# Two graph layers on one core: POOL's large operations in pieces, a played order, and the loads' place in their queue

## The chip, the cores and the metric

The kernel runs on one core of a Trainium2 chip. The metric is the device time of one execution in microseconds (us), as the median of several runs. The core has five engines that work side by side, each through its own instructions in order: PE (matrix multiplications), DVE (vector operations), ACT (activations and copies), POOL (a second, slower vector engine) and SP, which here issues transfers. Engines wait for each other through semaphores.

## The reference

A batch of 128 graphs with 128 nodes each has node features x (64 numbers) and an adjacency matrix adj. Two layers follow each other, each with a residual and a normalization:

```python
# layer 0
mask = (adj > 0.0)
xj_proj = x @ W1[:F]
diff = x[:, :, None, :] - x[:, None, :, :]
h = relu(xj_proj[:, :, None, :] + diff @ W1[F:] + b1)     # F = 64, H = 192
hm = einsum('bjkh,bjk->bjh', h, mask)
deg = sum(mask, axis=-1)
x = layernorm(x + hm @ W2 + deg[..., None] * b2)
# layer 1
agg = einsum('bmn,bnd->bmd', adj, x)
h = elu(agg @ V1 + c1)
h = elu(h @ V2 + c2)
x = layernorm(x + h @ V3 + c3)
```

About 6% of adj is positive, so a node has few neighbours, and h is needed for those alone.

## The kernel before, in words

Graphs are worked on in 64 pairs. For a pair the kernel sorts the nodes by degree and gives each block of nodes (BLOCKS) as many neighbour slots as its largest node should need. The slots of a pair make nine units of 66 to 170 columns. A dense path at the end (`dense`) takes pairs with larger degrees than the slots allow; on these inputs it only looks whether there are any.

For each pair p these steps are generators, run as threads:

- `load` issues two transfers on SP's queue (adj and xx, L498 and L500), three pairs ahead (AHEAD).
- `prepare` makes the mask mk and the degrees on DVE (L511), degb and keyc on POOL (L518, L519), spreads them on PE (L524, L526), ranks them (cmp, L533) and makes the permutation permb (L541) on DVE.
- `sort_x` makes permf on ACT (L552), sorts x on PE (L556), copies it to xsT (L560), projects it (L570) and adds the bias to make aj (L577, ACT). POOL then makes sa (L584) and corr (L603); between them stand a product on PE (L589, L591) and ea on DVE (L596).
- `sort_mask` sorts the mask on PE (L612, L615), copies it on ACT (mtp L620, permT L622), takes prefix sums (L626), copies them to vp (L629) and makes the one-hot matrices oh on DVE (L636), one for each unit.
- `turn` transposes adj and x on PE (L651, L652) and copies them (turned, L656). `project_c` projects (L669, L672) and splits the result cp into three bf16 parts: ACT makes the first (L679), DVE the rest r (L683), ACT the second (L686), POOL the third (L688).
- `unit`, nine times, copies aj into one of four PSUM banks e (L811, ACT), gathers onto it on PE with 18 matmuls (L823) and reduces it to sums on DVE (L832). It is the bulk of the work.
- `finish` makes hm on POOL (L741), projects it (L746 to L753), brings it back to the order of the nodes (ys L757, L763), normalizes it to x (y L696, st L701 on DVE; ve L708, rs L709, nb L712 on POOL; apply L719 on ACT), aggregates (L770, agg L774) and runs layer 1 (L778 and L780, L786 and L787, L792 and L794, with exponentials e L729 on ACT and h L732 on DVE) up to the last normalization and the transfer of o (L798).

Sorting, gathering and aggregating are matmuls of 64 columns, marked "PE:t"; the others use all 128.

The order of all instructions is made when the program is built, by `Flow`. It keeps a clock for each engine, and for a resource called PORT that POOL's operations and oh on DVE both take. A thread offers its next step with a planned cost and the events that it needs; a step can be issued from the time when all of them are there. Among the steps for the engine of the earliest one that could start within NEAR (NEAR_PE on PE) of it, `Flow` takes the one with the smallest due time. A change of mode on PE adds SWITCH to the planned time and HOLD to the due time. The due time of a thread starts at `due(p, step)` = ROUND (p - AHEAD) + STEP step and grows by STEP with each step; units use PACE = ROUND / 9, and are also held to it by the time at which the first one ran (T0). Due times only choose among steps: on the chip there are no clocks, only the order and the semaphores.

Four further PSUM banks m are handed out by `Flow` for everything else. The constants have threads of their own: `arrive` (weights on ACT's queue), `arrive_next` (b1, b2 on SP), `arrive_late` (seven transfers of v2, v3, v1 and the biases on SP, L236), `consts_pool` (slotc L351, srow L357, v1p L360), `consts_dve`, `consts_w` (wc L398, L403, the sums copy L405, the product L411, L414), `consts_b2` (POOL, L328 to L332) and `consts_late` (w2d L452, v1p L457, slots L463, L471, rows L474 and on). Before the threads run, the loads of pairs 0 to 2 are issued, then `arrive_late`, and only then do the first lanes start, which issue the load of pair 3.

Of the kernel before, what the change touches and what calls it, by code (L numbers as in the profile page):

```python
# [87 lines left out]
class Flow:  # L88
# [11 lines left out]
    NEAR_PE = 0.05  # L100
    SWITCH = 0.1
    HOLD = 5
# [8 lines left out]
    def start(self, due, pace, gen):  # L111

        self.serial += 1
        th = [due, self.serial, pace, gen, None]
        self._next(th, None)

    def _next(self, th, got):
        try:
            th[4] = th[3].send(got)
        except StopIteration:  # L120
            if th in self.threads:
                self.threads.remove(th)
            return
        if th not in self.threads:
            self.threads.append(th)
        elif got is not None:
            th[0] += th[2]
# [50 lines left out]
def sparse(tc, env):  # L178
# [6 lines left out]
    NE = 4  # L185
# [7 lines left out]
    ROUND = 11.39  # L193
    AHEAD = 3
    PACE = ROUND / NB
    STEP = 1.94
    TURN = 4
    CS = 3
    SORT = 5
    FIN = 0.5  # L200

    def due(p, step):
        return ROUND * (p - AHEAD) + STEP * step

    def pace(u):
        return PACE * u

# [25 lines left out]
    const, temp = g.const, g.const  # L233

# [72 lines left out]
    def arrive_next():  # L307
        halves(nc.sync, b1c, g.b1, [[1, HB], [HB, 3]])
        fetch(b2r, bass.AP(tensor=g.b2.tensor, offset=g.b2.offset, ap=[[0, P], [1, O]]))
        happened([6.0], "const", "b1")  # L310
        happened([6.0], "const", "b2")

    def arrive_late():
        fetch(v2s, g.v2)
        fetch(v3s, g.v3)
        for s in range(2):
            fetch(v1d[s * F:(s + 1) * F], g.v1)
        for c, lo, times in ((g.c1, 0, 1), (g.c2, H1, 1), (g.c3, 2 * H1, 2)):
            n = c.shape[0]
            fetch(rows[:, lo:lo + times * n].rearrange("p (t n) -> p t n", t=times),  # L320
                  bass.AP(tensor=c.tensor, offset=c.offset, ap=[[0, P], [0, times], [1, n]]))
        happened([14.0], "const", "v")
        happened([14.0], "const", "c")
# [12 lines left out]
    def consts_pool():  # L336
# [11 lines left out]
        flow.start(0.1, 0.1, consts_prefix(below))  # L348
        yield from op("POOL", 0.2, lambda: v.memset(b2p, 0.0), "b2p0")
# [8 lines left out]
        yield from op("POOL", 1.0, scale, "srow")  # L358
        for s in range(2):
            yield from op("POOL", 0.3, lambda: v.memset(v1p[:, s], 0.0), f"v1p0{s}")  # L360
# [9 lines left out]
    def consts_dve():  # L370
# [8 lines left out]
        yield from op("DVE", 0.4, lambda: v.memset(wad, 0.0), "wad0")  # L379

# [121 lines left out]
    def prepare(p):  # L502
# [42 lines left out]
        flow.start(due(p, SORT), STEP, sort_x(p, ev))  # L545
        flow.start(due(p, SORT), STEP, sort_mask(p, ev))

# [16 lines left out]
    def project_a(p, xsT, ev):  # L564
# [19 lines left out]
        evs, = yield ("POOL PORT", 0.95, [have] + made("srow"), 0, lambda: nc.gpsimd.tensor_mul(sa, aj, srow))  # L584
# [18 lines left out]
        ev, = yield ("POOL PORT", 1.05, [ev, evs], 0, lambda: nc.gpsimd.tensor_sub(corr, ea, sa))  # L603
# [41 lines left out]
    def turn(p):  # L645

        d, a, xx = S[p], ADJ[p], XX[p]

        def transpose(t):
            for s in range(2):  # L650
                nc.tensor.transpose(t[:, s * N:(s + 1) * N], a[:, s, :], ident)  # L651
            nc.tensor.transpose(t[:, 2 * N:3 * N], flat(xx), ident)  # L652
        ev, t = yield ("PE", 0.4, [event("load", p)] + made("ident"), 1, transpose)
        turned = d["turned"] = prep.tile([P, 3, N], F32, name="turned", bufs=9)
        ev, = yield ("ACT", act(3 * N), [ev], 0,
                     lambda: nc.scalar.copy(flat(turned), t[:, :3 * N]))  # L656
        flow.give(t, ev)
        happened(ev, "turned", p)
        flow.start(due(p, CS), STEP, project_c(p, ev))

    def project_c(p, ev):
# [19 lines left out]
        for s in range(2):  # L681
# [5 lines left out]
        ev, = yield ("POOL PORT", 1.12, [ev], 0,  # L687
                     lambda: nc.gpsimd.tensor_sub(cp[:, 2], r1, cp[:, 1]))  # L688
# [47 lines left out]
    def finish(p):  # L736
# [3 lines left out]
        ev, = yield ("POOL PORT", 1.05, [event("corr", p)] + [event("sums", p, i) for i in range(NB)], 0,  # L740
                     lambda: nc.gpsimd.tensor_sub(hm, d["sums"], d["corr"]))  # L741
# [97 lines left out]
    def begin(p):  # L839
        if p < NP:  # L840
            load(p)
            happened([max(flow.clock.values(), default=1.0 + p) + 2.5], "load", p)
            flow.start(due(p, 0), STEP, prepare(p))
            flow.start(due(p, TURN), STEP, turn(p))
# [3 lines left out]
    def lane(u, ev):  # L848
        p = units[u][0]
        if p not in begun:  # L850
            begun.add(p)
            begin(p + AHEAD)
            flow.start(ROUND * (p + FIN), STEP, finish(p))
        ev = yield from unit(u, ev)
        if u + NE < len(units):
            flow.start(pace(u + NE), PACE, lane(u + NE, ev))

    nc.vector.memset(mone, -1.0)
    for p in range(min(AHEAD, NP)):
        begin(p)  # L860
        if p == 0:
            arrive_next()
    arrive_late()
    flow.start(-101.0, 0.1, arrive())
    flow.start(-100.0, 0.1, consts_pool())
    flow.start(-99.0, 0.1, consts_dve())
    flow.start(-98.0, 0.1, consts_w())
    flow.start(-97.0, 0.1, consts_wad())
    flow.start(-96.0, 0.1, consts_b2())
    flow.start(-95.0, 0.1, consts_banks())  # L870
    flow.start(ROUND * -0.5, 1.0, consts_late())
    for k in range(NE):
        flow.start(pace(k), PACE, lane(k, [0.0]))
# [217 lines left out]
```

## Time and profile before

| | us |
|---|---|
| median of 3 runs | 790.31 (789.89 to 790.33) |
| the profiled execution | 789.11 |
| its span in the trace | 787.3 |
| PE busy | 756.4 (96%) |
| DVE busy | 736.8 (94%) |
| ACT busy | 661.6 (84%) |
| POOL busy | 441.7 (56%) |
| gathers, L823 on PE | 376.4, 10368 matmuls |
| reductions, L832 on DVE | 345.6, 576 operations |
| oh, L636 on DVE | 168.3, 576 operations |
| cp, L688 on POOL | 74.8, 64 operations of 128x512 |
| hm, sa, corr (L741, L584, L603) on POOL | 64.3, 64.1, 64.0, 64 operations of 128x384 each |

A busy time is the time in which an engine works on something; what lies between the span and it is idle time, for which the trace names the event that ended it. PE's ends are modelled, so distances between starts say more about PE than durations do. Tables by stretches give, for each engine, the busy time within a stretch of the span. The chain of work that ended last is 91% PE.

### The profile page before, as it was taken

The page shows a single profiled execution, that of the slowest core. Times are in us where ns is not written, and L with a number is a line of the kernel's source. Part 1 is how long each engine was busy: PE and PEld are TensorE (multiplying, and loading weights), DVE is VectorE, ACT ScalarE, POOL GpSimd, SP SyncE. Part 2 cuts the span into 40 slices and gives each one's busy share as a digit, 9 for nine tenths or more (in the row PEclk, how much of TensorE's full clock was granted, in tenths as well). Part 3 has the DMA queues.
Part 4 walks back from the last instruction along what each step waited for, and adds up shares of the span by engine and source line. Part 5 has one row for each costly group of instructions (what it writes and reads, how often), then busy time and mean ns, then how long its engine had stood idle before and what let it go on. Part 6 is the DMA issues. An engine that isn't in the chain of part 4 may idle for free.

```text
span 787.3 us, 35836 instructions
## 1 busy us (share of the span) xinstructions
PE 756.4 (96%) x14551; PEld 684.9 (87%) x14552; DVE 736.8 (94%) x2421; ACT 661.6 (84%) x1862; POOL 441.7 (56%) x806
## 2 busy tenths in 40 slices
PE   4889999999999999999999999999999999999994
PEld 2578999999999999999999999999999999999983
DVE  3899999999999999999999999999999999999982
ACT  1868889898989989898998989889898988989862
POOL 4445556555655655565565556556556655655542
PEclk9999999999999999999999999999999999999996
DMA  3000101101101110110111011011101101110000
GB/s 95 2 2 23 27 22 27 30 20 30 26 20 30 27 29 20 30 27 20 30 27 29 21 30 26 20 30 26 30 20 31 26 20 30 27 28 21 9 9 14
DMA packets 63884, 19.91 MB, mean 25 GB/s; under 512 B 46560, under 2 KB 63712, under 8 KB 63712
## 3 DMA queue, kind: packets, MB, share of 16 engines
q1 hardware_dynamic: 63008, 17.25, 9.4%
q8 instruction: 116, 1.90, 1.0%
q14 instruction: 56, 0.46, 0.2%
q10 hardware_dynamic: 704, 0.30, 0.1%
HBM read 13.27 MB, written 4.19 MB: 22 GB/s over the span
## 4 chain that ended last, share of the span: by engine, by line
PE 91%; DVE 4%; ACT 1%; DMA 1%; issue 1%; SPq 1%; POOL 1%; ACTq 0%; POOLq 0%; DVEq 0%
PE e L823 43%; PE m L570 6%; PE m L746 6%; PE m L669 5%; PE m L780 4%; PE m L794 4%; PE m L787 4%; PE m L763 4%; PE m L770 2%; PE m L556 2%; PE m L651 2%; PE m L750 1%; PE m L672 1%; PE m L589 1%; DVE sums L832 1%; DVE oh L636 1%
## 5 line engine op out<-in xcount | busy, mean ns | idle before, releaser
L823 PE MATMUL e<-oh,cp 128*64 128x162 bf16 (+3 forms) x10368 | 376.4, 228 | 5.4 <-ACT e L811 3.8
L823 PEld LDWEIGHTS <-cp 128*64 128x64 bf16 x10368 | 349.1, 110 | 24.4 <-issue 16.9
L832 DVE TENSOR_REDUCE sums<-e 128x54 f32<-128x486 f32 (+8 forms) x576 | 345.6, 610 | 4.2 <-PE e L823 1.9
L811 ACT COPY e<-aj 128x504 f32<-128x504 f32 (+6 forms) x576 | 300.2, 549 | 17.0 <-DVE sums L832 11.6
L636 DVE TENSOR_TENSOR oh<-vp,slotc 128x336 bf16<-128x336 bf16 (+6 forms) x576 | 168.3, 321 | 0.7 <-PE e L823 0.5
L688 POOL TENSOR_TENSOR cp<-r,cp 128x512 bf16<-128x512 f32 x64 | 74.8, 1170 | 73.8 <-ACT cp L686 73.7
L709 POOL TENSOR_TENSOR rs<-ve,mhalf 128x2 f32<-128x2 f32 x128 | 89.2, 697 | 10.6
L577 ACT ACTIVATE aj<-m,b1c 128x128 f32<-128x128 f32 x192 | 56.5, 365 | 34.7 <-PE m L570 34.6
L741 POOL TENSOR_TENSOR hm<-sums,corr 128x384 f32<-128x384 f32 x64 | 64.3, 1004 | 31.1 <-DVE sums L832 31.1
L518 POOL CAST degb<-deg 128x2 bf16<-128x2 f32 x64 | 12.4, 193 | 122.5 <-DVE mk L511 122.5
L584 POOL TENSOR_TENSOR sa<-aj,srow 128x384 f32<-128x384 f32 x64 | 64.1, 1001 | 15.6 <-ACT xsT L560 8.3
L603 POOL TENSOR_TENSOR corr<-ea,sa 128x384 f32<-128x384 f32 x64 | 64.0, 1001 | 11.2 <-DVE ea L596 11.2
L679 ACT CAST cp<-m 128x256 bf16<-128x256 f32 x128 | 41.6, 376 | 33.3 <-PE m L672 33.2
L729 ACT ACTIVATE e<-m,mone 128x256 f32<-128x256 f32 x128 | 60.7, 474 | 6.7 <-PE m L787 3.7
L708 POOL TENSOR_SCALAR ve<-st 128x2 f32<-128x2 f32 x128 | 24.5, 191 | 67.1 <-DVE st L701 61.6
L732 DVE SCALAR_TENSOR_TENSOR h<-e,m 128x256 f32<-128x256 f32 x128 | 53.0, 414 | 5.5 <-ACT e L729 5.5
L570 PE MATMUL m<-xsT,wad 128*128 128x128 f32 x384 | 57.6, 287 | 0.5 <-DVE h L732 0.5
L746 PE MATMUL m<-w2d,hm 128*128 128x128 f32 x384 | 54.3, 278 | 0.0
L683 DVE TENSOR_TENSOR r<-m,cp 128x256 f32<-128x256 f32 x128 | 48.5, 419 | 5.8
L719 ACT ACTIVATE x<-y,nb,rs 128x64 f32<-128x64 f32 x128 | 51.1, 464 | 0.9 <-POOL nb L712 0.8
L570 PEld LDWEIGHTS m<-xsT,wad 128*128 128x128 f32 x384 | 48.7, 194 | 0.9 <-DVE h L732 0.7
L746 PEld LDWEIGHTS m<-w2d,hm 128*128 128x128 f32 x384 | 48.0, 192 | 1.1 <-POOL hm L741 0.2
(147 smaller groups left out, 1416.6 us busy)
## 6 DMA issues: line engine op xcount, KB each, us to landing
adj<-in_adj_dram SPq DMA_DIRECT2D x64, 128.0 KB, 2.4
xx<-in_x_dram SPq DMA_DIRECT2D x64, 64.0 KB, 2.1
out_dram<-o SPq DMA_DIRECT2D x64, 64.0 KB, 1.6
degs<-ys SPq DMA_DIRECT2D x64, 1.0 KB, 1.6
w1s<-in_L_gnn_W_dram ACTq DMA_DIRECT2D x2, 96.0 KB, 3.1
rows<-in_L_gnn_b_dram SPq DMA_DIRECT2D x3, 64.0 KB, 3.4
w2s<-in_L_gnn_W_dram ACTq DMA_DIRECT2D x2, 48.0 KB, 2.7
v2s<-in_L_gnn_W_dram SPq DMA_DIRECT2D x1, 64.0 KB, 2.3
```

The lines of the kernel that those rows point to most:

```text
L570: nc.tensor.matmul(aps[:, c * N:(c + 1) * N], wad[:, c, :], xsT, start=True, stop=True)
L584: evs, = yield ("POOL PORT", 0.95, [have] + made("srow"), 0, lambda: nc.gpsimd.tensor_mul(sa, aj, srow))
L603: ev, = yield ("POOL PORT", 1.05, [ev, evs], 0, lambda: nc.gpsimd.tensor_sub(corr, ea, sa))
L636: lambda: nc.vector.tensor_tensor(oh[:, :, c].rearrange("p b (s w) -> p b s w", w=w), vp[:, :, p0:p1].rearrange("p b (o w) -> p b o w", o= ...
L688: lambda: nc.gpsimd.tensor_sub(cp[:, 2], r1, cp[:, 1]))
L709: nc.gpsimd.tensor_tensor(rs, ve, mhalf, op=OP.pow)
L729: lambda: nc.scalar.activation(e, z, AF.Exp, bias=mone))
L741: lambda: nc.gpsimd.tensor_sub(hm, d["sums"], d["corr"]))
L746: nc.tensor.matmul(yb[:, :2 * O], hm[:, c, :], flat(w2d[:, c]), start=(c == 0), stop=False)
L811: lambda: nc.scalar.copy(e.rearrange("p (c s w) -> p c s w", c=3, w=w), d["aj"][:, :, p0:p1].rearrange("p c (o w) -> p c o w", o=1) .to_br ...
L823: nc.tensor.matmul(e[s * HB:(s + 1) * HB, c * n:(c + 1) * n], cp[:, k, s, c * HB:(c + 1) * HB], oh[:, s, base:base + n], start=False, stop ...
L832: nc.vector.tensor_reduce(d["sums"][:, :, p0:p1], e.rearrange("p (c s w) -> p c w s", c=3, w=w), AX.X, OP.add, apply_absolute_value=True)
```

## The change

It has five parts.

1. POOL's four large operations of a pair are issued in pieces: sa, corr and hm (384 columns) in three of 128, the third part of cp (2 x 256 columns) in four of 128. Each piece is a step of its own, with a planned cost of 0.42 in place of 0.95 to 1.12.
2. The due times come from a table DUE, one number for each step of each kind of thread, counted from ROUND p; ROUND goes from 11.39 to 11.21. A thread no longer has a due time that grows evenly. NEAR_PE goes from 0.05 to 0.03 and HOLD from 5 to 4.9.
3. The planned arrival of a load comes from a running clock of SP's queue (`queued`) instead of a fixed distance from the engines' clocks.
4. `arrive_late`, the seven transfers of late constants, is issued after the first lanes have started, so behind the load of pair 3.
5. Of the constants' threads, those for slotc, srow, b2p and v1p on POOL, and those from mtwoh on on DVE, become threads of their own with later due times; the memset of b2p comes after srow.

What is computed stays as it is. The diff, cut to its core:

```diff
-    NEAR_PE = 0.05
+    NEAR_PE = 0.03
     SWITCH = 0.1
-    HOLD = 5
+    HOLD = 4.9
...
-    def start(self, due, pace, gen):
+    def start(self, base, due, gen):
 
         self.serial += 1
-        th = [due, self.serial, pace, gen, None]
+        th = [0.0, self.serial, gen, iter(due), None, base]
         self._next(th, None)
...
+        th[0] = th[5] + next(th[3], th[0] - th[5])
         if th not in self.threads:
             self.threads.append(th)
-        elif got is not None:
-            th[0] += th[2]
...
-    ROUND = 11.39
+    ROUND = 11.21
...
+    DUE = {
+        "prepare": (-34.01, -32.27, -30.23, -29.85, -25.33),
+        "sort_x": (-13.14, -15.45, -7.19, -8.98, -19.88, -5.52, -3.51, -2.52, 0.83, 1.06, 7.6,
+                   4.57, 6.95),
...
+        "finish": (15.58, 20.81, 18.39, 20.56, 21.58, 23.28, 25.11, 26.72, 28.25, 29.18, 28.09,
+                   29.43, 35.25, 38.97, 38.77, 39.45, 41.87, 43.65, 44.61, 47.29, 53.63, 49.35,
+                   55.17),
+        "unit": (0, -6.28, 2.48),
+    }
...
+    def begin_thread(name, p, gen):
+        flow.start(ROUND * p, DUE[name], gen)
...
+    SP = [0.7]
+
+    def queued(cost):
+
+        SP[0] = max(SP[0], max(flow.clock.values(), default=0.0)) + cost
+        return [SP[0] + 2.6]
...
-        evs, = yield ("POOL PORT", 0.95, [have] + made("srow"), 0, lambda: nc.gpsimd.tensor_mul(sa, aj, srow))
+
+        for c in range(3):
+            evs, = yield ("POOL PORT", 0.42, [have] + made("srow"), 0,
+                          lambda: nc.gpsimd.tensor_mul(sa[:, c], aj[:, c], srow[:, c]))
...
-        ev, = yield ("POOL PORT", 1.05, [ev, evs], 0, lambda: nc.gpsimd.tensor_sub(corr, ea, sa))
+        for c in range(3):
+            evs, = yield ("POOL PORT", 0.42, [ev, evs], 0,
+                          lambda: nc.gpsimd.tensor_sub(corr[:, c], ea[:, c], sa[:, c]))
...
-        ev, = yield ("POOL PORT", 1.12, [ev], 0,
-                     lambda: nc.gpsimd.tensor_sub(cp[:, 2], r1, cp[:, 1]))
+        for s in range(2):
+            for h in range(2):
+                part = slice(h * cols // 2, (h + 1) * cols // 2)
+                evl, = yield ("POOL PORT", 0.42, [ev], 0,
+                              lambda: nc.gpsimd.tensor_sub(cp[:, 2, s, part], r1[:, s, part],
+                                                           cp[:, 1, s, part]))
...
-        ev, = yield ("POOL PORT", 1.05, [event("corr", p)] + [event("sums", p, i) for i in range(NB)], 0,
-                     lambda: nc.gpsimd.tensor_sub(hm, d["sums"], d["corr"]))
+        have = [event("corr", p)] + [event("sums", p, i) for i in range(NB)]
+        for c in range(3):
+            ev, = yield ("POOL PORT", 0.42, have, 0,
+                         lambda: nc.gpsimd.tensor_sub(hm[:, c], d["sums"][:, c], d["corr"][:, c]))
...
             load(p)
-            happened([max(flow.clock.values(), default=1.0 + p) + 2.5], "load", p)
-            flow.start(due(p, 0), STEP, prepare(p))
-            flow.start(due(p, TURN), STEP, turn(p))
+            happened(queued(1.0), "load", p)
+            begin_thread("prepare", p, prepare(p))
+            begin_thread("turn", p, turn(p))
...
-    arrive_late()
-    flow.start(-101.0, 0.1, arrive())
...
-    for k in range(NE):
-        flow.start(pace(k), PACE, lane(k, [0.0]))
+    flow.start(-101.0, [0.0], arrive())
...
+    for k in range(NE):
+        flow.start(pace(k), DUE["unit"], lane(k, [0.0]))
+    arrive_late()
     flow.run()
```

## The prediction

> **What bounds the kernel now.** I read the page's busy shares first (PE 96%, DVE 94% of 787.3 us), then the busy time of the engines by stretches, cut where PE's idle time changes. After the two times of a stretch come the busy times of PE, weight loads, DVE, ACT and POOL.
>
> ```profile
> 0.00:9.10 9.10, 5.50 (x20) 2.89 (x21) 5.51 (x41) 2.35 (x5) 7.69 (x41) 1.00 0.48 115
> 9.10:16.20 7.10, 0.03 (x1) 0.00 (x0) 0.75 (x4) 0.48 (x1) 0.27 (x2) 1.00 0.42 109
> 16.20:33.50 17.30, 15.00 (x107) 10.47 (x107) 11.71 (x51) 11.92 (x39) 5.22 (x10) 1.00 0.02 4
> 33.50:60.00 26.50, 21.69 (x472) 18.74 (x474) 26.00 (x78) 18.00 (x46) 12.99 (x15) 1.00 0.01 3
> 60.00:100.00 40.00, 39.36 (x743) 35.55 (x739) 38.22 (x126) 34.48 (x97) 23.16 (x43) 1.00 0.11 26
> 100.00:745.00 645.00, 644.91 (x12742) 592.08 (x12739) 631.11 (x2067) 574.53 (x1627) 379.36 (x673) 1.00 0.11 25
> 745.00:764.70 19.70, 19.20 (x426) 17.88 (x421) 17.62 (x44) 13.65 (x34) 6.59 (x12) 1.00 0.07 13
> 764.70:787.30 22.60, 10.70 (x63) 7.26 (x61) 5.87 (x19) 6.24 (x18) 6.38 (x15) 0.67 0.06 13
> ```
>
> From 100 to 745 us PE is idle for 0.09 us: a round of one pair takes 11.49 us (the same row of the timeline returns at that distance) and PE is its only bound, DVE being at 631.11/645 = 97.8%. The change leaves PE's matmuls as they are. So it can win only what PE loses at the ends: 3.6 + 7.1 + 2.3 + 4.8 + 0.6 us up to 100 us, and 12.4 us after 745. The largest piece, 9.1 to 16.2 us, has a name in the list of waits:
>
> ```profile
> PE m L651 <- DMA adj<-in_adj_dram: 8.5, 2, 7.1
> DVE mk L511 <- DMA adj<-in_adj_dram: 8.7, 4, 6.3
> ```
>
> Third column: the longest wait, 7.1 us, for the adj of pair 3. The timeline of SP's queue says why it is late:
>
> ```profile
> 5.85 0.47 SPq L500 DMA_DIRECT2D xx<-in_x_dram  x1
> 6.37 0.47 SPq L236 DMA_DIRECT2D v2s<-in_L_gnn_W_dram  x1
> 6.88 0.43 SPq L236 DMA_DIRECT2D v3s<-in_L_gnn_W_dram  x1
> 7.35 1.14 SPq L236 DMA_DIRECT2D v1d<-in_L_gnn_W_dram  x2
> 8.53 1.53 SPq L236 DMA_DIRECT2D rows<-in_L_gnn_b_dram  x3
> 10.11 0.47 SPq L498 DMA_DIRECT2D adj<-in_adj_dram  x1
> ```
>
> Seven constants are issued ahead of pair 3. Its transposes stand early in PE's in-order queue, with L411 and the keys of pair 0 (L524) behind them, so pair 0 itself waits for pair 3. In the stretch 33.5 to 60 the bound is another: DVE is busy 26.0 of 26.5 us and PE loses 4.8.
>
> The rows for POOL and its port:
>
> ```profile
> L688 POOL TENSOR_TENSOR cp<-r,cp 128x512 bf16<-128x512 f32 x64 | 74.8, 1170 | 73.8 <-ACT cp L686 73.7
> L329 POOL TENSOR_TENSOR hm<-b2r,hi 128x64 f32<-128x64 f32 x1 | 0.3, 307 | 0.0
> ```
>
> ```profile
> 32.20 2.50 POOL L688 TENSOR_TENSOR cp<-r,cp 128x512 bf16<-128x512 f32 x2 [2.75 <-ACT cp L686]
> 32.52 1.17 DVE L636 TENSOR_TENSOR oh<-vp,slotc 128x336 bf16<-128x336 bf16 x1
> ```
>
> The second pair is the lock: an oh takes a median of 0.32 us, but 1.17 when it starts inside POOL's cp.
>
> **What the skill says.** "SBUF — State Buffer", section "SBUF: two separate sides": DVE operations with two SBUF inputs and POOL operations share a port pair, as an exclusive lock held for the whole instruction. The trace agrees (the 1.17 us above). "GPSIMD Engine Reference", section 3.1: a two-input operation on POOL costs about 2.6 cycles an element; at the 1.2 GHz that the section reckons with, an estimate of 0.83 us for 384 columns. The trace has 1.001, so some 0.17 is fixed, and shorter pieces pay it more often. "TensorE: Matmul & The Clock Gate", Part 1: PE starts at half its clock and warms after about 3.4 us of sustained work. The trace agrees in kind: six matmuls of L570 take 1.59 us at 23.4 and 0.89 at 26.5.
>
> **The change, part by part.** Sums are made against the profiled execution: span 787.3, own time 789.1, which is 1.2 below the median of 790.3; I subtract the same difference from the median.
>
> *Loads' order and the start.* The order of instructions of the new kernel has load 3 right behind load 2, so its adj is issued at 6.37 in place of 10.11. Adj of pairs 1 and 2 landed 3.0 and 2.9 us after issue (4.35 to 7.33, 5.34 to 8.2), so I expect it at 9.3. The seven constants move back by two issues (1.0 us). Who waits for them: v1p on ACT, which now stands between xsT and vp of pair 0, near 13.5 us, while v1d should be in by 9.5 + 3.0 = 12.5; L471 on PE and L474 on DVE come later. I take 0, at most 1.0 if v1d is late, since vp is behind it. PE's queue now has L411 and the keys of pair 0 ahead of the transposes of pairs 1 to 3. The chain by old durations: sums copy ends about 7.45 (DVE has prefix, wc 0.40, wad 0.70, mk 0.4, w2d 0.69, copy 0.54 from 4.7 on), L411 1.54, wc 0.22, keys and their latency 0.5, cmp 0.54, permb 0.5: permb of pair 0 near 11.2 against 20.2. POOL's degb of pair 0 moves ahead of the v1p and b2p constants (7.07 to about 6.3), and mk moving behind wc and wad is hidden, as POOL's slotc runs until 5.8. From permb to the first complete gather was 20.2 to 33.5, 13.3 us. It then falls near 23 to 25. But PE reaches it with one L669 and one L570 fewer done (0.70 + 0.67), so not all of 9 is gained. As DVE bounds the ramp, I check with its account: DVE idle before 60 us was 3.6 + 6.3 + 5.6 + 0.5 = 16.0. In the new chain I count 4.1 of waits up to 14.5 us (0.8 before its first operation, 0.7 for w1s, 1.5 for L411, 1.1 for the keys of pairs 0 to 2 and vp of pair 0) and allow 3.4 for later ones (vp of pair 1, cp of pair 0): 7.5. Gain 8.5, from 6 to 11.
>
> *Pieces.* Thirteen POOL operations replace four. Each: between 1.001/3 = 0.33 (no fixed part) and, from the rows of 64 and 384 columns, 0.307 + 64 x 2.17 ns = 0.45. I take 0.45. Per pair 13 x 0.45 = 5.8 against 1.17 + 3 x 1.00 = 4.2, so POOL goes from 441.7/64 = 6.9 to 8.5 of 11.4 us: 74%, hidden beside PE. A blocked oh loses at most 0.45 instead of 0.85. In the ramp three were blocked (32.5, 36.8, 70.8), for 2.5 us of a bound DVE: gain 1.0, from 0 to 1.5. Between 100 and 745 no oh was blocked, so there is nothing to gain there.
>
> *Order in the round.* Counting changes between 64-column and full matmuls in the new order, there are four in a round as before, about 0.1 us each by start distances. The gathers go 5 and 4 together in place of 8 and 1, which leaves more time to refill the four e banks. One wait of 0.054 us after L570 in each old round (start to start 0.723 for 0.670) may go: -3.1 over 57 rounds. New waits are possible. The tightest that I find by laying the old durations along the new order: x of layer 0 is ready at about 8.35 us of the round and PE wants it at 8.55 (L770); the bank for L570 is free 0.4 ahead. What is queued behind L770 is the whole of PE. I take -0.5; from -3 to +12, the last being 0.2 a round.
>
> *Tail.* The last pair's chain after its last gather was 22.6 us. In the new order PE's work behind the last gather, by steady start distances, is 2 x 0.90 (L746 to L753) + 2 x 0.45 + 2 x 0.22 + 3 x 0.55 + 4 x 0.54 + 4 x 0.50 = 8.95, against 6.0 before. 2.9 us of other pairs' work moves under a chain that leaves PE idle for half its time, so the last gather comes that much sooner; the two last pairs now interleave, which I price at 0.9. Gain 2.0, from 0 to 2.9. NEAR_PE and HOLD act on the order alone and are contained in it.
>
> Sum: -8.5 - 1.0 - 0.5 - 2.0 = -12.0: 777.1 for the profiled execution, 778.3 for the median.
>
> **Rivals.** *The round grows* (slower): more POOL instructions, each with its own wait, make x's factors or an oh late in every round, and PE stands at L770. For it: x's 0.2 us of slack, POOL at 74%, factors of 1.64 us in the trace (ve, rs, nb) where the kernel plans 1.24. Against it: hm and cp have over 1 us, and DVE has 2% spare. The other 12 us are eaten from 12/57 = 0.21 us a round; at 0.4 it is 778.3 + 23 = 801. *The start is given back*: DVE, busy 26.0 of 26.5 in the ramp, keeps PE waiting whatever came earlier; start and pieces give 3, tail 2: 785.3. *It does nothing*: the wait for adj is only the first of several and L411, b2p or vp end at the old time; 790.
>
> **How the numbers follow.** Forecast 0.66, round grows 0.14, start given back 0.14, nothing 0.06. A measurement of this kernel can tell about 0.2% (1.6 us) from no change. Faster 0.66 + 0.14 = 0.80, same 0.06, slower 0.14. The range: low from the gains at their ends (11 + 1.5 + 3 + 2.9 = 18.4 gives 771.9, cut to 773), high to 788.5, past the rival at 785 and short of the other two.
>
> **What would show it.** Right: adj of pair 3 issued near 6.4, no PE wait over 2 us after 8 us, first gather complete by 25, PE idle for under 0.2 us between 100 and 745, last gather to end 22 to 24 us. Wrong: rounds over 11.6 us with PE waiting at L770 for ACT or at L746 for POOL; or DVE full and PE losing over 8 us between 25 and 60.

## The result, and the profile after

| us | before | after |
|---|---|---|
| median | 790.21 (789.89 to 790.33, 4 runs) | 785.09 (784.65 to 787.08, 4 runs) |
| ratio, 95% interval | | 0.9941, 0.9923 to 0.9959 |
| the profiled execution | 789.11 | 785.48 |
| its span | 787.3 | 783.6 |
| PE busy | 756.4 (96%) | 764.4 (98%) |
| PE idle (span less busy) | 30.9 | 19.3 |
| POOL busy | 441.7 (56%) | 527.6 (67%) |
| one round (median distance of the same row) | 11.494 | 11.663 |

The kernel became 5.1 us faster by the medians (3.6 between the two profiled executions, of which the one before lies 1.1 below its median); 12.0 were forecast. The table says where the rest is. PE's idle time fell by 11.6 us, nearly what the forecast had in sum. But PE's busy time rose by 8.0 us, though it does the same 14551 matmuls. The difference of the two is that of the spans, 3.7 us (the last digit is rounded).

These are the stretches of the kernel after, cut as before (the last stretch ends 0.36 us behind the span); after the two times come PE, weight loads, DVE, ACT and POOL.

```profile
0.00:9.10 9.10, 5.41 (x23) 3.43 (x25) 5.98 (x38) 1.87 (x4) 6.61 (x34) 1.00 0.47 116
9.10:16.20 7.10, 6.33 (x48) 5.13 (x47) 5.71 (x37) 5.48 (x18) 3.64 (x15) 1.00 0.29 75
16.20:33.50 17.30, 15.88 (x226) 12.16 (x224) 14.48 (x49) 13.43 (x38) 8.04 (x18) 0.80 0.03 9
33.50:60.00 26.50, 25.22 (x500) 21.44 (x500) 25.95 (x82) 19.80 (x51) 16.18 (x43) 1.00 0.10 25
60.00:100.00 40.00, 40.00 (x771) 36.00 (x772) 39.11 (x130) 35.69 (x102) 27.39 (x71) 1.00 0.09 21
100.00:745.00 645.00, 644.99 (x12555) 581.30 (x12550) 629.43 (x2039) 566.24 (x1602) 448.75 (x1161) 1.00 0.11 25
745.00:764.70 19.70, 19.66 (x409) 18.14 (x405) 15.83 (x38) 13.38 (x34) 11.55 (x30) 1.00 0.05 9
764.70:784.00 19.30, 6.87 (x42) 4.52 (x41) 5.16 (x17) 6.25 (x19) 5.46 (x14) 0.74 0.08 19
```

Up to 100 us PE is idle for 7.2 us (3.69 + 0.77 + 1.42 + 1.28 + 0), where it was 18.4. The hole of 7.1 us is gone. Behind 745 us it is idle for 12.1 (0.04 + 12.43, less the 0.36), nearly as before (12.4). The sixth line is the surprise: PE is full in both kernels, but in the same 645 us the kernel after gets through 12555 matmuls, the kernel before through 12742. A full engine can still be slower; the busy share doesn't show it. A matmul of L595 stands in the trace with 275 ns, while the next one starts 112 ns behind it, so a gap of 0.1 us between two starts is covered and counts as busy.

The queue of SP has the load of pair 3 where it was expected, ahead of the constants:

```profile
6.23 0.47 SPq L523 DMA_DIRECT2D adj<-in_adj_dram  x1
...
7.26 0.47 SPq L252 DMA_DIRECT2D v2s<-in_L_gnn_W_dram  x1
```

How the lead comes and goes is seen from the ends of the 576 reductions (L832 before, L870 after), after less before: the first -8.9 us, the 36th -13.6, the 54th -12.8, the 301st -10.4, the 501st -6.8, the last -4.8. So the start won 12.8 up to the 54th, the rounds gave back 8.0, and the end behind the last reduction is 1.2 longer (23.0 for 21.8).

**Where the round grew.** As ends of matmuls are modelled, I go by distances between starts, from the first matmul of a group to the first of the next. Each group has a distance that it takes when a group of its own form follows; what is more is the price of the change or a wait. The form stands in the lines: 128*128 is a full matmul, 128*64 one of 64 columns, 64*128 one of 64 rows. This is one run of full matmuls of the kernel after, on PE:

```profile
300.73 0.42 PE L581 MATMUL m<-permf,xx 128*64 128x128 f32 x4
301.08 0.23 PE L830 MATMUL m<-rowp,onesb 128*128 128x128 bf16 x1
...
301.60 0.61 PE L801 MATMUL m<-ys,permT 128*128 128x64 f32 x4
302.14 0.70 PE L700 MATMUL m<-wc,turned 64*128 64x256 f32 x4
...
303.40 0.87 PE L595 MATMUL m<-xsT,wad 128*128 128x128 f32 x6
304.20 0.90 PE L861 MATMUL e<-oh,cp 128*64 128x168 bf16 x20
```

And this is where project_c stood in the kernel before, directly behind the 64-column gathers:

```profile
401.57 0.97 PE L823 MATMUL e<-oh,cp 128*64 128x162 bf16 x32
402.46 0.70 PE L669 MATMUL m<-wc,turned 64*128 64x256 f32 x4
```

project_c's first part (L700, before L669) is neither full nor of 64 columns: it is the only step of 64 rows, which the description of the kernel doesn't name as a form of its own. Behind gathers it takes part in a change that is due anyway. Behind L801 it makes one of its own: L801 to L700 is 540 ns, and L801 takes 447 when a full matmul follows (L763 to L570 in the kernel before). The table has the medians over some 54 rounds, in ns:

| change | before | after |
|---|---|---|
| 64-column steps to the first run of full matmuls | L823 to L669: 402 - 286 = 116 | L581 to L830: 356 - 220 = 136 |
| to project_c inside a run | none | L801 to L700: 540 - 447 = 93 |
| first run to gathers | L615 to L823: 205 - 112 = 93 | last matmul of L595 to L861: 205 - 110 = 95 |
| 64-column steps to the second run | L823 to L589: 783 - 655 = 128 | L808 to L549: 356 - 220 = 136 |
| second run to gathers | L652 to L823: 202 - 109 = 93 | L646 to L861: 205 - 112 = 93 |
| sum | 430 | 553 |

(286, 655 and 220 are the distances of the same gathers and of the fp32 steps L581 and L808 when a step of 64 columns follows. The change back from 64 rows to full matmuls, L669 to L672 and L700 to L703, takes 635 ns in both kernels and is left out.) The difference is 123 of the 169 ns. Beside it, weights that are loaded late cost 39 ns at L595 and 33 at L784, each between the first matmul of the group and the second. At L595 the first weights are loaded 43 ns behind the signal of y on DVE, which gives back a bank; what L784 waits for isn't shown. In the kernel before, the step of L595 (there L570) lost 53 ns at the same place, the step of L784 (L746) nothing. That makes 19 ns more, and small differences add 27.

### The profile page after: what moved, and what is told of

The parts are those of the page before. It is cut to its first block, busy times and chain, and to the rows that moved or that the text cites. A ratio compares the mean times of both kernels' runs of the same rounds, so it can differ in the third digit from the quotient of the medians.

```text
span 783.6 us, 36480 instructions
## 1 busy us (share of the span) xinstructions
PE 764.4 (98%) x14551; PEld 682.1 (87%) x14552; DVE 741.7 (95%) x2421; ACT 662.1 (84%) x1862; POOL 527.6 (67%) x1382
## 4 chain that ended last, share of the span: by engine, by line
PE 94%; DVE 2%; DMA 1%; ACT 1%; POOL 0%; issue 0%; SPq 0%; ACTq 0%; POOLq 0%
PE e L861 44%; PE m L595 6%; PE m L784 6%; PE m L700 5%; PE m L818 4%; PE m L801 4%; PE m L832 4%; PE m L825 3%; PE m L581 2%; PE m L808 2%; PE m L682 2%; PE m L549 2%; PE m L788 1%; PE m L703 1%; PE m L830 1%; PE m L657 1%
## 5 line engine op out<-in xcount | busy, mean ns | idle before, releaser
L849 ACT COPY e<-aj 128x504 f32<-128x504 f32 (+6 forms) x576 | 315.6, 560 | 62.2 <-DVE sums L870 60.7
L861 PE MATMUL e<-oh,cp 128*64 128x162 bf16 (+3 forms) x10368 | 365.2, 228 | 0.5 <-DVE oh L667 0.3
L861 PEld LDWEIGHTS <-cp 128*64 128x64 bf16 x10368 | 344.0, 110 | 16.3 <-issue 1.4
L870 DVE TENSOR_REDUCE sums<-e 128x54 f32<-128x486 f32 (+8 forms) x576 | 345.5, 610 | 8.3 <-PE e L861 1.6
L722 POOL TENSOR_TENSOR cp<-r,cp 128x128 bf16<-128x128 f32 x256 | 108.3, 443 | 139.9 <-ACT cp L717 139.9
L667 DVE TENSOR_TENSOR oh<-vp,slotc 128x336 bf16<-128x336 bf16 (+6 forms) x576 | 170.6, 331 | 10.2 <-PE e L861 8.6
L633 POOL TENSOR_TENSOR corr<-ea,sa 128x128 f32<-128x128 f32 x192 | 87.2, 455 | 51.3 <-DVE ea L624 51.3
L779 POOL TENSOR_TENSOR hm<-sums,corr 128x128 f32<-128x128 f32 x192 | 88.4, 461 | 10.2 <-DVE sums L870 5.6
L612 POOL TENSOR_TENSOR sa<-aj,srow 128x128 f32<-128x128 f32 x192 | 85.3, 459 | 4.8 <-ACT aj L602 4.8
L765 ACT ACTIVATE e<-m,mone 128x256 f32<-128x256 f32 x128 | 64.2, 501 | 3.1 <-PE m L825 2.2
L595 PE MATMUL m<-xsT,wad 128*128 128x128 f32 x384 | 56.9, 285 | 0.2 <-ACT permT L653 0.2
L784 PE MATMUL m<-w2d,hm 128*128 128x128 f32 x384 | 55.5, 281 | 0.0
L595 PEld LDWEIGHTS m<-xsT,wad 128*128 128x128 f32 x384 | 48.3, 193 | 1.0 <-ACT vp L660 0.3
L784 PEld LDWEIGHTS m<-w2d,hm 128*128 128x128 f32 x384 | 47.8, 191 | 0.7
L700 PE MATMUL m<-wc,turned 64*128 64x256 f32 x256 | 45.7, 432 | 0.0
L717 ACT CAST cp<-r 128x512 bf16<-128x512 f32 x64 | 42.9, 670 | 0.2 <-DVE r L714 0.2
```

The lines of the kernel that those rows point to most:

```text
L595: nc.tensor.matmul(aps[:, c * N:(c + 1) * N], wad[:, c, :], xsT, start=True, stop=True)
L612: lambda: nc.gpsimd.tensor_mul(sa[:, c], aj[:, c], srow[:, c]))
L633: lambda: nc.gpsimd.tensor_sub(corr[:, c], ea[:, c], sa[:, c]))
L667: lambda: nc.vector.tensor_tensor(oh[:, :, c].rearrange("p b (s w) -> p b s w", w=w), vp[:, :, p0:p1].rearrange("p b (o w) -> p b o w", o= ...
L700: nc.tensor.matmul(cps[s][:, :cols], d["turned"][k, 2, :], wc[k, :], start=True, stop=False)
L722: lambda: nc.gpsimd.tensor_sub(cp[:, 2, s, part], r1[:, s, part], cp[:, 1, s, part]))
```

## The experiments

The changed kernel is planned by `Flow` like the one before. In most experiments the order of steps that `Flow` had chosen was written down and played back, so that every instruction keeps its place on its engine except for the step named and, where it is said, copies that go with it. The edits of an order are shown as a diff of that order. Line numbers in an experiment's profile are those of its own text; tiles tell the steps apart. Each median has its own runs of the kernel before beside it (790.0 to 790.3), to which the ratios refer.

### The start: load 3 alone, and the rest of the order

Load 3 alone, put into the kernel before:

```diff
-    arrive_late()
     flow.start(-101.0, 0.1, arrive())
...
         flow.start(pace(k), PACE, lane(k, [0.0]))
+    arrive_late()
     flow.run()
```

> The kernel before with its own order on every engine; only the late constants are issued behind load 3 on SP's queue. Theory A (two thirds of the start's gain is the place of load 3, the rest the order in which PE, DVE and ACT take the first steps): the wait for adj of pair 3 falls from 7.1 us to under 1, and 4 to 6.5 us are gained, 784 to 786. Rival 1 (the place of the load is all of the gain): 8.5 or more, under 782. Rival 2 (the order alone matters, since the next wait stands behind this one): under 2 us, over 788.

Measured: 782.89 (781.56 to 783.83), ratio 0.9910 (0.9898 to 0.9923). Seven transfers moved past one load win 7.1 us, more than the whole change. The lead is 6.2 us at the first reduction and 6.1 at the last, at a round of 11.493. The other 1.4 us are at the end of the profiled execution (20.4 us behind the last reduction for 21.8), where no edit is but the granted clock differs: it falls to half 14.8 us before the end in the kernel before and 8.5 us before it here, and the same four matmuls, L780 there and L875 here, take 1.22 and 0.71 us:

```profile
773.89 1.22 PE L780 MATMUL m<-agg,v1p 128*128 128x128 f32 x4
```

```profile
767.49 0.71 PE L875 MATMUL m<-agg,v1p 128*128 128x128 f32 x4
```

The adj of pair 3 is issued at 6.29 and lands at 9.51, 3.2 us later; behind the constants it took 6.0 us (10.11 to 16.10). PE no longer waits for it, as the theory had it; the longest wait for an adj on PE's list, 1.9 us, is for pair 1.

The opposite, in the changed kernel:

```diff
+    arrive_late()
     flow.start(-101.0, [0.0], arrive())
...
-    arrive_late()
     flow.run()
```

> The changed kernel with its own order on every engine; only the late constants go ahead of load 3 on SP's queue again. Theory A (the load's place is worth most of the start, but with L411 and the keys of pair 0 ahead of pair 3's transposes part is kept): 2 to 5 us more than the changed kernel, 787 to 790. Rival 1 (the load's place is all): 6.5 us or more, over 791.5. Rival 2 (the order alone matters): under 1 us more, under 786.

Measured: 792.82 (791.9 to 793.88), ratio 1.0038 (1.0025 to 1.0050): 7.7 us above the changed kernel, and PE waits 6.7 us for adj of pair 3 again (the third column is the longest wait):

```profile
PE m L791 <- DMA adj<-in_adj_dram: 6.7, 1, 6.7
```

Both directions give 7 to 8. The first lies between the theory and rival 1, the second is what rival 1 said: the place of the load is most of the start.

The start of the changed kernel ahead of the old rounds, with POOL's operations whole:

```diff
-order before, step 1 to the end
+order after, steps 1 to 142 (up to about the first gathers)
+order before, without the steps that are done
```

> The start of the changed kernel in front of the rounds of the kernel before: the kernel before, with its four whole POOL operations, in which the first 142 steps (up to about the first gathers) come in the order of the changed kernel, load 3 is issued ahead of the late constants, and all other steps keep the order of the kernel before. Theory A (the change gains 9 to 13 us at the start, and its new order in the rounds gives 9 back): the first reduction ends near 26.1 us, a round is 11.49 again, and the time is 790.2 - 9 to 790.2 - 12.8, so 777.5 to 781. Rival (the start's lead cannot be kept, as DVE bounds the ramp whatever the rounds are): 784 to 786.

Measured: 782.61 (780.79 to 784.55), ratio 0.9906 (0.9890 to 0.9921). The lead is 7.2 us at the first reduction, 7.7 at the 54th and 7.3 at the last, with a round of 11.493: what the start wins is kept in full when the rounds are the old ones. It is 1.6 us short of the theory, since the changed kernel's lead grows to 13.6 us in its ramp and this one's doesn't. PE is idle in 33.5 to 60 us for 1.3 us in the changed kernel, 1.5 with load 3 back in its old place, but 4.0 here and 2.6 with load 3 alone. So some 4 us of the lead come from the changed ramp. Most of it is its order, not the pieces: with the changed order and whole operations (the last run under "The pieces") the lead still grows from 9.4 us at the first reduction to 13.1 at the 36th, for 8.9 and 13.6 with pieces. Which of its steps do it wasn't tried.

### The round: moving project_c

```diff
 order on PE in 54 rounds
 L581
+L700 L703 (project_c)
 L830 L832 L801
-L700 L703 (project_c)
 L816 L818 L595
```

> The changed kernel with its own order of instructions, in which one step is moved: in 54 rounds project_c's two matmuls (L700, L703), with the copies that follow them, come first in their run of full matmuls, directly behind the 64-column run, in place of behind the gathers of L832 and L801. Theory A (the round grew by matmul shape changes, of which this is a fifth in each round, measured at 94 ns between L801 and L700): 54 x 0.094 = 5.1 us less, about 780.0, round 11.57 against 11.66. Theory B (the round grew by POOL's pieces, their waits and their lock): no change, 785 within 1. Theory C (the order is in balance by DVE and PE only looks full): no change or slower, since the banks are taken earlier.

Measured: 796.34 (795.66 to 798.17), ratio 1.0079 (1.0065 to 1.0093), a round of 11.898: 11 us slower than the changed kernel where 5 less were expected. L581 to project_c is 353 ns, the same as to any full matmul, so the change of its own is gone. But project_c takes two of the four banks m 1.1 us sooner, and the steps behind it now wait for those that y gives back: L801 to L816 is 545 ns for 447, L818 to L595 662 for 447, and the gather behind L595 comes 61 ns later still. In all 54 rounds both steps start 42 ns behind the signal of y. In this timeline of DVE and PE (PEld is the loading of weights; L843 is y, L927 the first product of layer 1, L706 the projection of x) PE starts as each y ends:

```profile
306.85 0.29 DVE L843 TENSOR_TENSOR y<-m,x 128x128 f32<-128x128 f32 x1 [0.17 <-PE m L943]
...
307.19 0.27 PE L927 MATMUL m<-onesb,rowp 128*128 128x256 bf16 x1
...
307.70 0.29 DVE L843 TENSOR_TENSOR y<-m,xx 128x128 f32<-128x128 f32 x1
308.05 0.30 PEld L706 LDWEIGHTS m<-xsT,wad 128*128 128x128 f32 x2 [0.33 <-DVE y L843]
```

The theory of the change is neither shown nor refuted by this; theory C is what happened.

```diff
 order on PE in 54 rounds, with the move above, and hm whole
-L861 (66 columns)  L581
+L581  L861 (66 columns)
...
-L808
 L861 (first gather of the next run)
+L808
```

> The changed kernel with its own order of instructions and four things moved in nearly every round: project_c's matmuls first in their run of full matmuls (as above); the permutation's transposes L581 ahead of the 66-column gather, so that the 64-column run begins behind bf16 gathers; the aggregation L808 behind the first gather of the next 64-column run; and hm as one POOL operation. Theory A: 54 x 0.094 + about 54 x 0.04 + 57 x 0.032 = 5.1 + 2.2 + 1.8 = 9.1 us less, about 776. Theory B (pieces cause the growth, of which only hm's are undone here): about 2 us less, 783. Theory C (a moved step only moves the wait): 784 to 787.

Measured: 796.48 (794.63 to 796.77), ratio 1.0072 (1.0059 to 1.0086), round 11.871. ACT's copy agg went with L808. The same two waits (545 and 662 ns) outweigh the rest.

The reverse in the kernel before:

```diff
 order on PE in 53 rounds
 L823 (66 columns)
-L669 L672 (project_c)
 L786 L787 L612 L615
+L669 L672 (project_c)
 L823 (168 columns)
```

> The kernel before with its own order of instructions, in which one step is moved: in 53 rounds project_c's two matmuls (L669, L672), with the copies behind them, stand behind the other full matmuls of their run instead of directly behind a run of gathers, as the changed kernel has it. Nothing else of the change is in it. Theory A (shape changes): 53 x 0.094 = 5.0 us more, about 795, with L669 starting 94 ns later behind the instruction ahead of it. Theory B (pieces): no change, 790 within 1.

Measured: 801.84 (801.6 to 802.79), ratio 1.0145 (1.0129 to 1.0160), round 11.687. L615 to L669 is 205 ns for 112, the 93 expected, but 90 more came at L778 (202 for 112). The two copies of cp behind project_c moved along with it on ACT (and the two r on DVE) and now stand ahead of the copy permT (L622), and in 55 rounds L778 starts 42 ns behind the signal of permT, which gives back a bank. Half fits the theory; the other half is a bank again.

So a run was made that changes a form and nothing else:

```diff
+    small64 = const([P, P], BF16, "small64")
...
+            v.memset(small64, 2.0 / P)
...
-            nc.tensor.matmul(key[:, 2 * N:3 * N], small, iotb, start=True, stop=True)
+            nc.tensor.matmul(key[:, 2 * N:3 * N], small64[:64], iotb[:64], start=True, stop=True)
```

> The kernel before with its own order on every engine and the same results; one bf16 matmul of each pair, L526, which stands between full matmuls (L524 ahead, L763 behind), takes 64 rows in place of 128 (its constant is 2/128 in place of 1/128). Theory A (PE loses about 94 ns at each change between full matmuls and matmuls of 64 rows or columns, whatever the order around it): L524 to L526 goes from 112 to about 205 ns, L526 to L763 from 56 to about 150, a round from 11.494 to 11.68, and 57 x 0.187 = 10.7 us are added, 801. Rival (the 94 ns ahead of project_c in the changed kernel are a wait for a bank or for turned, and a change costs nothing by itself): 790 within 1, both distances as before.

Measured: 804.20 (803.43 to 805.65), ratio 1.0176 (1.0162 to 1.0191). First the kernel before, then this one, on PE:

```profile
406.94 0.28 PE L524 MATMUL m<-identb,degb 128*128 128x128 bf16 x2
407.05 0.22 PE L526 MATMUL m<-iotb,small 128*128 128x128 bf16 x1
407.11 0.61 PE L763 MATMUL m<-ys,permT 128*128 128x64 f32 x4
```

```profile
416.44 0.28 PE L528 MATMUL m<-identb,degb 128*128 128x128 bf16 x2
416.65 0.23 PE L530 MATMUL m<-iotb,small 64*128 64x128 bf16 x1
416.80 0.66 PE L767 MATMUL m<-ys,permT 128*128 128x64 f32 x4
```

The distances go from 112 to 207 ns and from 56 to 157, and the next (L763 to L570) from 447 to 495: 95 + 101 + 48 = 244. The round grew by 246, to 11.740, and PE's busy time in 100 to 745 us is 645.00. Half the rows, the same columns, the same order and banks: the change of form alone costs 95 ns on the way in, as ahead of project_c, and 149 on the way back to fp32, where the theory had 94 (so 14.2 us were added for 10.7). The rival is refuted.

Last, the same price made smaller in the changed kernel:

```diff
 order on PE in 54 rounds
 L861 (162 columns)
+L581
 L861 (66 columns)
-L581
 L830
```

> The changed kernel with its own order, in which one step is moved in 54 rounds: the transposes L581 (fp32, 64 columns) go ahead of the 66-column gather, so that the run ends in bf16 gathers. Theory A (a change to full matmuls costs 136 ns behind fp32 and 116 ns behind bf16): the stretch from the 162-column gather to L830 falls from 1.280 to 1.258 us, 1.2 us less in all, about 783.9; a round of 11.64. If the change costs the same behind both: 785.1. If L581 then waits for permf: more.

Measured: 782.61 (781.86 to 783.1), ratio 0.9901 (0.9885 to 0.9916), against 0.9941 (0.9923 to 0.9959) of the changed kernel. The stretch falls from 1.280 to 1.249 us, 31 ns for the 22 expected. L784 to L788 loses 32 more (703 to 671), and L595 to the next gather takes 29 more (804 to 833). The round is 11.631. The first is the theory's; why the wait at L784 went and that at L595 grew is not settled.

### The pieces

hm alone as one operation, in the changed kernel:

```diff
-        for c in range(3):
-            ev, = yield ("POOL PORT", 0.42, have, 0,
-                         lambda: nc.gpsimd.tensor_sub(hm[:, c], d["sums"][:, c], d["corr"][:, c]))
+        ev, = yield ("POOL PORT", 1.0, have, 0,
+                     lambda: nc.gpsimd.tensor_sub(hm, d["sums"], d["corr"]))
```

> The changed kernel with its own order of instructions, and hm as one POOL operation of 384 columns in place of three of 128. Theory A (shape changes, plus 0.032 us a round in which PE waits between L784 and L791 for a later piece of hm): 57 x 0.032 = 1.8 us less, about 783.3. Theory B (POOL's pieces are the main cause of the longer round): more than 3 us less, 782 or under. If one whole hm ends later than the three pieces would let the first projection begin, it is slower by up to 0.3 us a round.

Measured: 785.14 (783.8 to 787.54), ratio 0.9930 (0.9916 to 0.9943). L784 to L788 is 708 ns for 703: hm's pieces are not what PE waits for there. My guess of 32 ns for them falls.

Pieces in the kernel before, each group in the place of its whole:

```diff
-tensor_mul(sa, aj, srow)
+for c in range(3): tensor_mul(sa[:, c], aj[:, c], srow[:, c])
...
 (likewise corr, the third part of cp, hm)
```

> The kernel before with its own order; only the four whole POOL operations of a pair are issued as thirteen pieces, each set in the place of its whole. Theory A (pieces cost POOL's time alone, and the round grew by matmul shape changes): round 11.49, 790.2 within 1.5, perhaps 1 less from DVE's ramp. Theory B (pieces lengthen the round by their waits, their lock or their fixed part): PE waits between the gathers or at L746, round of 11.6 or more, 796 to 800.

Measured: 817.90 (817.79 to 818.66), ratio 1.0354 (1.0341 to 1.0367), round 11.986. Neither theory had 28 us. The gather of 66 columns starts 1107 ns behind the one ahead of it, for 630. This is the chain on POOL, ACT and PE (rs is a factor of o, L924 the copy of e):

```profile
402.59 0.80 POOL L820 TENSOR_TENSOR rs<-ve,mhalf 128x2 f32<-128x2 f32 x1
403.43 0.59 ACT L830 ACTIVATE o<-y,rs 128x64 f32<-128x64 f32 x2 [0.42 <-POOL rs L820]
404.06 0.33 ACT L924 COPY e<-aj 128x198 f32<-128x198 f32 x1
404.44 0.35 PE L936 MATMUL e<-oh,cp 128*64 128x66 bf16 x11 [0.29 <-ACT e L924]
```

Three pieces of sa take 1.28 us where the whole takes 1.00; rs stands behind them on POOL, o waits for rs, and the copies of e stand behind o on ACT. (The planner also gave other banks m to about a ninth of the matmuls here; in the next run the banks are those of the kernel before.) To see if that is all, the factors of o were put ahead of sa:

```diff
 order on POOL in 57 rounds, with pieces
+ve rs (of o)
 sa sa sa
-ve rs (of o)
```

> The kernel before with its own order and the four POOL operations in pieces in the place of the wholes (as the earlier run with pieces alone), with one move: in 57 rounds the factors of the last normalization (ve, rs of o) go ahead of sa's three pieces on POOL instead of behind them. Theory A (the 0.49 us that a round grew came from ACT standing at o for rs, which stood behind sa's longer pieces, with the e copy queued behind o on ACT and the 66-column gather behind that on PE): the wait is gone, a round is 11.49 to 11.55, and the time is 790 to 794. Theory B (the pieces cost through their number or the port lock wherever they stand): 805 to 818.

Measured: 806.16 (805.62 to 807.77), ratio 1.0201 (1.0187 to 1.0215), round 11.816. ACT's wait for rs is gone from the list, and the 66-column gather is still late (906 ns). And sa's pieces lie beside four oh, and two oh in each round take over 0.5 us; the mean of an oh went from 315 to 377 ns. Nine of those are 0.56 us a round on an engine that had 0.25 to spare, which leaves 0.31; the round grew by 0.32, and DVE is busy for 638.95 of 645 us. It is between the two theories: the wait was real, and without it the lock shows. That the lock makes the whole 0.32 is this sum, not a chain of waits that was followed.

All four operations whole, in the changed order:

```diff
-for c in range(3): tensor_mul(sa[:, c], aj[:, c], srow[:, c])
+tensor_mul(sa, aj, srow)
...
 (likewise corr, the third part of cp, hm, each at the place of its first piece)
```

> The changed kernel with its own order, and all four POOL operations whole, each at the place of its first piece. Theory A (in the new order the pieces neither cost PE time nor buy it): round 11.66, 784 to 787. Rival (the new order can be kept only with pieces, as factors and other short POOL steps stand between them): PE waits for POOL's results in every round, 790 or more.

Measured: 813.74 (812.56 to 814.23), ratio 1.0296 (1.0282 to 1.0310), round 12.116. The rival is right, by another way than it says. On DVE, POOL and PE (L801 here is the second part of project_c, L908 the first product of layer 1):

```profile
407.53 0.99 POOL L731 TENSOR_TENSOR corr<-ea,sa 128x384 f32<-128x384 f32 x1 [1.35 <-DVE ea L724]
407.91 0.82 DVE L765 TENSOR_TENSOR oh<-vp,slotc 128x336 bf16<-128x336 bf16 x1
...
408.64 0.27 DVE L826 TENSOR_TENSOR y<-m,x 128x128 f32<-128x128 f32 x1
...
408.97 0.27 PE L908 MATMUL m<-onesb,rowp 128*128 128x256 bf16 x1
```

An oh beside the whole corr takes 0.82 us, y behind it comes late, and PE stands at L908 until y gives its bank back (281 ns for 68), and 214 more at the projection of x. Against the wholes at these places, pieces are worth 0.45 us a round in this order; they cost 0.49 in the old one. Each order was fitted to the lengths of POOL's operations that it was made for.

### One wait of the kernel before

```diff
 order on PE in 56 rounds, with load 3 ahead of the constants
 L570
-L626
 L651 L652
+L626
```

> The kernel before with its own order, load 3 issued ahead of the late constants (782.9 by itself), and one step moved in 56 rounds: L626 goes behind the transposes L651 and L652 in place of ahead of them. At L626 PE stood 0.053 us in every round for the bank that y on DVE gives back. Theory A (the wait is that of the bank, and the transposes take one that is free sooner): 56 x 0.053 = 3.0 us less, 779.9, round 11.44. Rival (the transposes then wait for the same bank): 782.9, round 11.49.

Measured: 783.14 (782.52 to 783.32), ratio 0.9910 (0.9895 to 0.9925), round 11.492. L570 to L651 is now 723 ns, as L570 to L626 was. That is the rival's number, but neither reading holds, since the 53 ns were never at L626. In both kernels they lie between the first and the second of L570's six matmuls (165 ns, the others 112 apart), and the step behind the last one starts on time (111 ns). What runs behind L570 can't change that. The signal of y comes 55 ns ahead of L570's first weight load, so a wait for y's bank isn't shown there either; what holds the second matmul stays open.

## Why the prediction was wrong

*Sign: right; the idle time in sum: in part luck.* The waits that the forecast removed at the start are gone, and PE's idle time fell by 11.6 us for a sum of 12.0. But the start gave more of it than forecast and the tail almost nothing, and the two errors cancel.

*Start and pieces in the ramp, -9.5:* -12.8 at the 54th reduction, -11.3 of PE's idle time. adj of pair 3 was issued at 6.23 (forecast 6.37) and landed at 10.2 (9.3), and the first complete gather was reduced at 26.1. DVE's idle time before 60 us, with which the forecast checked this term, fell from 16.0 to 7.9 us (7.5 forecast). Two runs put 7 to 8 us on the load alone, so the split of two thirds and one third with which I went into the experiments was off on both sides: the order at the very start adds little (7.4 for 7.1), the order of the ramp about 4. The term for pieces, -1.0, is not shown by itself: pieces in the old order won 0.7 us between the first and the 18th reduction and then lost more; in the new order the lead at the 36th is 0.5 us larger with them than without.

*Order in the round, -0.5: this step failed.* It said "Counting changes between 64-column and full matmuls in the new order, there are four in a round as before". That count is right and is not the one that matters. project_c, with 64 rows, is a third form, and I took it for a full one. Before, it stood behind steps of 64 columns in 59 of 64 pairs and shared their change; after, it stands behind full matmuls in 62. Its own change costs 93 ns a round, the other four 30 more (both runs now begin behind fp32 steps), late weights and small differences 46; in place of -0.5 the rounds gave +8.0. The wait of 0.054 us that the term hoped to win "after L570" was misread: it lies inside L570. The Trainium skill has the rule that the forecast left out: "TensorEngine Tiling (Array Packing)", section "Tiling Modes", says that changing the tiling mode, and not merely the tile, drains TensorE, and it lists 128x64 and 64x128 as modes of their own. It gives no price; the trace agrees with 93 to 149 ns a change. The planner has the same blind spot: to `Flow`, project_c is plain PE, so it can move it behind full matmuls for nothing.

*Rival "the round grows":* the time was between it and the forecast, and its price (0.17 of the 0.21 us from which it decides) came true, but not its mechanism. PE did not wait for x's factors or for oh in the changed kernel. The mechanism is real all the same: in the old order it made the round 0.49 us longer.

*Rival "the start is given back":* its 785.3 is nearly the measured time, by luck. The start was not given back: in the ramp, 33.5 to 60 us, PE idles for 1.3 us where it idled for 4.8.

*Tail, -2.0: not won.* PE is idle for 12.1 us behind 745, for 12.4 before. The last reduction is 4.8 us earlier, the end 3.6. Why the rest of this term didn't come wasn't tried; the clock doesn't explain it, since the granted half lasts for the last 9.8 us of the kernel after and the last 14.8 of the kernel before.

*POOL's rows:* a piece took 0.443 to 0.461 us (0.45 forecast).

**What is faster than both.** Three versions take 782.6 to 782.9 us: the kernel before with load 3 moved; the same with the changed order at the start; and the changed kernel with L581 a gather earlier. They are not told apart by these runs. A table of due times made by a planner that knows three forms on PE, which could keep the changed kernel's ramp and lose project_c's own change, wasn't tried.

## What to carry to other kernels

When an engine is full, count its instructions in an equal stretch of time before and after: here a busy share of 100% hid a slower engine. List the form of every matmul (rows and columns) in its order, and count changes between all forms. An order planned to the tenth of a microsecond belongs to the durations and costs it was planned with: to move one step, or to cut one operation, ask which bank, which port and which queue it takes earlier or longer, since each of these brought a new wait in these runs.

## What the runs showed that I had not expected

- A bf16 matmul of 64 rows between full ones costs 95 ns on the way in and, with fp32 behind it, 101 + 48 on the way back, though it has the same 128 columns to stream.
- The port lock that the Trainium skill describes in "SBUF — State Buffer", section "SBUF: two separate sides", reaches PE through banks: an oh of 0.82 us beside a whole corr, and PE 0.21 us later at a step that has nothing to do with either.
- One load issued behind seven constants cost 7 us of 790: it was issued 3.8 us later and then took 6.0 us to land for 3.2.
- The granted clock at the very end differs between executions: with it at half for 14.8 us instead of 8.5, the last stretch was 1.4 us longer.
